# Two cross-attention layers: column sums by block transposes and one 0/1 matmul, weights' sums by a column of ones

## The chip, the core and the metric

The kernel runs on one core of a Trainium2 chip. A core has TensorE (PE: matrix products and transposes, results in PSUM banks), VectorE (DVE), ScalarE (ACT), GpSimd (POOL) and SyncE (SP, here used to issue transfers), and 16 DMA engines. Every engine works through its own queue of instructions in order and waits for the others by semaphores. The metric is the time of one launch on the device in microseconds; lower is better. All data are fp32.

## What is computed

`x` is 8 x 100 x 1024, the context `ctx_512` is 8 x 1444 x 512. Two layers of single-head attention from `x` to the context; hidden width 1024. Cut to what matters:

```python
# layer 0
Q = x @ Wq + bq;  K = ctx @ Wk + bk;  V = ctx @ Wv + bv
w = softmax(Q @ K.T / 32, axis=-1)          # over the 1444 keys
x = x + (w @ V) @ Wo + bo
# layer 1, with weights of its own
w = softmax(q @ k.T / 32, axis=1)           # over the 100 queries
x = x + w @ v
out = (x - mean(x)) * rsqrt(var(x) + 1e-6) * gamma + beta
```

In layer 1 the softmax goes over the queries, so the weights of a query do not add up to 1 over the keys, and the value bias has to be multiplied with their sum.

## The kernel before

**Shape of the work.** The kernel never forms keys and values. It multiplies the weights first: `wqk0` = Wq Wk^T (1024 x 512), `wvo` = Wv Wo (512 x 1024), `wqk1`; then the queries times these (`queries`), scores of the queries against the raw context, the weighted rows of the context, and a projection. A weight product is done by `weight_products` (L187) as seven half-size products X, Z, Y, W and so on, whose operands are sums and differences formed on VectorE (`combine`, L135), and whose results ScalarE copies (`put`, L242) and VectorE adds (L247). The body (L376 on) does qk0, vo0, the queries of layer 0, qk1, then layer 0's attention for eight batches, the projection `project0`, the queries of layer 1, and layer 1's attention with its projections and the final normalisation.

**Order.** PE runs in the order in which the program is written (`manual_schedule(engines={PE})`). The instructions of the other engines are put in order by the framework's planner. SP issues nearly all loads. They go into a ring of ten buffers, `unit` (L72), 128 x 1536 elements each: weight rows first, then, for each batch, four units of context columns (`cT`) and four of context rows (`c`, three chunks of 120 rows of 512 elements, `load_rows`, L429). A load waits until PE has used what the buffer held before.

**Biases.** Four vectors come out of biases and weights: u (bq by Wk), wqbk (bk by Wq), for each layer, and for the output bias bv by Wo. `accumulate` (L251) multiplies each of the eight 128-row slices of a weight with a column of the bias and adds them up on VectorE, which leaves an accumulator of 128 partitions by 512 or 1024 columns. Its sum over the partitions is wanted, laid out as a column of 128 partitions for each 128 columns. `totals` (L301) does that: PE transposes each 128 x 128 block into a PSUM bank, and VectorE reduces along the free axis (L308). The key bias of layer 0, `c0`, is the same with `key_bias_sums` (L323): VectorE adds up xT times wqbk over the eight chunks for 400 tokens at once, and the sums over partitions are taken by eight transposes in L400. `bias_product` (L311) multiplies bq and bk and sums them over partitions with a matmul by ones, once for each layer. ScalarE adds the output bias to xT in L406.

**Attention of layer 0.** `scores0` (L475) makes the scores of one batch in 11 pieces of 131 or 132 keys, 3 in a bank, 44 matmuls; ScalarE takes them out (L501), VectorE the maxima (L502), and the softmax goes on in ScalarE. VectorE transposes the weights by 32 x 32 blocks (L523). For batches 0 and 7 PE transposes the first four chunks (`first_transposed`, L533). `weighted_rows` multiplies the context rows by the weights (L458, 48 matmuls). In the loop of L800 a batch's weighted rows alternate on PE with the scores of the batch two ahead; batches 0 and 1 have their scores alone (L794 to L799).

**Attention of layer 1.** `scores1` (L603) and `attend1` (L659) alternate in the same way. `attend1` multiplies w (100 queries as columns) by context rows, four matmuls of 128 columns for each of 12 chunks, into one bank from the second pool of PSUM; batches 6 and 7 use `weighted_rows`. `weight_sums` (L632) adds the weights over the chunks on VectorE, and `weight_totals` (L643) transposes the result on PE and reduces it to the sum for each query, `r`, which `untransposed` multiplies with the value bias (L731).

**The end.** `normalise` (L739) has mean and variance, a power on GpSimd for `rstd` (L745), and for the last batch two VectorE instructions of 512 columns (L754), each followed by a DMA (L755), one issued by SP, one by ScalarE.

Of the kernel before, what the change touches and what calls it, by code (L numbers as in the profile page):

```python
# [30 lines left out]
P = 128  # L31
# [10 lines left out]
CUTS = [S * n // NP for n in range(NP + 1)]  # L42
QD = 32
# [10 lines left out]
def two_layer_cross_attention(ctx: ExitStack, tc: tile.TileContext, a: dict, out: bass.AP):  # L54
# [17 lines left out]
    def unit(name):  # L72
        return stream.tile([P, E + L], F32, tag="unit", name=name)
# [18 lines left out]
    make_identity(nc, ident)  # L92
    mhalf = const.tile([P, 1], F32, tag="mhalf", name="mhalf")
# [93 lines left out]
    def weight_products(name, left, right, l_width, r_width, scaled):  # L187
# [10 lines left out]
        if name == "qk0":  # L198
# [3 lines left out]
            for h in range(1, EC):  # L202
                nc.sync.dma_start(out=units[h][:, :lh], in_=lsrc[:, h, :lh])
                nc.sync.dma_start(out=units[h][:, l_width:], in_=rsrc[:, h, :])
                if h == 1:
                    nc.sync.dma_start(out=units[0][:, l_width + rh :], in_=rsrc[:, 0, rh:])
# [3 lines left out]
        else:  # L210
            for h in range(EC):
                nc.sync.dma_start(out=units[h][:, :l_width], in_=lsrc[:, h, :])
                nc.sync.dma_start(out=units[h][:, l_width:], in_=rsrc[:, h, :])
# [37 lines left out]
        def accumulate(side):  # L251
            for v, of in scaled:
# [8 lines left out]
                for h in range(EC):  # L261
                    src = units[h][:, :l_width] if side == 0 else units[h][:, l_width:]
# [38 lines left out]
    def totals(name, acc, n):  # L301

        got = const.tile([P, n], F32, tag=name, name=name)
        for c in range(0, n, 4):
            ps = bank(f"{name}_{c}")
            for i in range(4):
                nc.tensor.transpose(ps[:, i * P : (i + 1) * P], acc[:, (c + i) * P : (c + i + 1) * P], ident)
            nc.vector.tensor_reduce(got[:, c : c + 4], ps.rearrange("p (c q) -> p c q", q=P), AX.X, ALU.add)  # L308
        return got

    def bias_product(layer):  # L311

        prod = small.tile([P, EC], F32, tag="bb", name=f"bb{layer}")
        nc.vector.tensor_tensor(prod, cols[f"L{layer}_xattn_bq"], cols[f"L{layer}_xattn_bk"], ALU.mult)
        part = small.tile([P, 1], F32, tag="bbs", name=f"bbs{layer}")
        nc.vector.tensor_reduce(part, prod, AX.X, ALU.add)
        ps = bank(f"bb_ps{layer}")
        nc.tensor.matmul(ps[:, 0:1], ones, part, start=True, stop=True)
        got = const.tile([P, 1], F32, tag=f"bqbk{layer}", name=f"bqbk{layer}")
        nc.vector.tensor_scalar(got, ps[:, 0:1], SCALE, None, ALU.mult)  # L320
        return got

    def key_bias_sums(name, t0, t1, wqbk):  # L323

        acc = work.tile([P, GT], F32, tag="kb", name=name, bufs=3)
        for k in range(EC):
            src = xT[:, k, t0:t1]
            if k == 0:
                nc.vector.tensor_scalar(acc, src, wqbk[:, k : k + 1], None, ALU.mult)
            else:  # L330
                nc.vector.scalar_tensor_tensor(acc, src, wqbk[:, k : k + 1], acc, ALU.mult, ALU.add)
# [53 lines left out]
    bqbk0 = bias_product(0)  # L385
    bqbk1 = bias_product(1)
    wvo, (acc_o,) = weight_products("vo0", "L0_xattn_WvT", "L0_xattn_Wo", L, E, (("L0_xattn_bv", 1),))
    u0 = totals("u0", acc_u, LC)
    wqbk0 = totals("wqbk0", acc_c, EC)
    nc.vector.tensor_tensor(out_bias, out_bias, totals("bvo", acc_o, EC), ALU.add)  # L390
    gT = [queries(0, wqk0, u0), None]
# [4 lines left out]
    c0 = const.tile([T, B], F32, tag="c0", name="c0")  # L396
    for g in range(B // G):
        ps = bank(f"c0_ps{g}")
        for i in range(G):
            nc.tensor.transpose(ps[:T, i * P : (i + 1) * P], kb0[g][:, i * T : (i + 1) * T], ident)  # L400
        nc.vector.tensor_reduce(
            c0[:, g * G : (g + 1) * G], ps[:T].rearrange("p (b q) -> p b q", q=P), AX.X, ALU.add
        )
    nc.vector.tensor_scalar(c0, c0, SCALE, bqbk0[:T], ALU.mult, ALU.add)
# [492 lines left out]
```

## Time and profile before

| | |
|---|---|
| median of three runs | 653.13 us (653.09 to 653.53) |
| the profiled execution | 653.41 us, its span 651.6 us |
| granted TensorE clock | 0.996 of full speed |
| busy in the span | PE 641.9, DVE 401.1, ACT 128.2, POOL 39.3 us |
| moved by DMA | 127.51 MB, 196 GB/s in the mean |

The profile is one execution. It gives the busy time of each engine, a row of 40 equal slices of the span (16.3 us each) in which a digit is the busy share in tenths, groups of instructions (line, engine, operation, destination <- source, partitions x elements, count | busy us, mean ns | idle time before), and the chain of work that ended last, followed back from the last instruction. A timeline lists single instructions with their start and length, and in brackets how long the engine had been idle before and what it was waiting for. PE is the multiplication itself, PEld the loading of its stationary operand, which overlaps it.

### The profile page before, as it was taken

How to read it: one execution, taken by the hardware profiler on the slowest of the kernel's cores; microseconds unless marked ns; L12 is line 12 of the kernel's file. 1: busy time of each engine (PE TensorE's matmuls, PEld its weight loads, DVE VectorE, ACT ScalarE, POOL GpSimd, SP SyncE). 2: the span in 40 equal slices, each digit the busy share in tenths (PEclk: the TensorE clock that was granted, in tenths of full speed). 3: DMA queues.
4: the chain of work that ended last, by engine and by line, in shares of the span. 5: the costliest groups of instructions: out<-in, count | busy, mean ns of one | idle time of the engine just before them, and what ended most of it. 6: DMA issues, size and time to landing. Idle time of an engine off the chain costs nothing.

```text
span 651.6 us, 10319 instructions
## 1 busy us (share of the span) xinstructions
PE 641.9 (99%) x4272; PEld 544.1 (84%) x4272; DVE 401.1 (62%) x764; ACT 128.2 (20%) x320; POOL 39.3 (6%) x44
## 2 busy tenths in 40 slices
PE   9999999999999999999999999999999999999994
PEld 7886445568899999999998555589999999999992
DVE  4979737996145775576662875268344433556984
ACT  1010010330203333312320000204232222310221
POOL 5000000000000000000000000000000000000763
PEclk9999999999999999999999999999999999999998
DMA  8937037000089788998999003029799998920122
GB/s 292 387 107 288 0 94 287 2 0 2 0 319 305 266 316 297 322 318 305 329 357 340 0 0 130 1 95 282 262 306 294 305 316 294 309 95 1 51 76 76
DMA packets 60236, 127.51 MB, mean 196 GB/s; under 512 B 3929, under 2 KB 22873, under 8 KB 60189
## 3 DMA queue, kind: packets, MB, share of 16 engines
q1 hardware_dynamic: 57742, 119.82, 53.9%
q0 software_dynamic: 2048, 6.56, 3.0%
q8 instruction: 33, 0.54, 0.3%
q10 hardware_dynamic: 398, 0.47, 0.2%
q14 instruction: 15, 0.11, 0.1%
HBM read 123.56 MB, written 3.28 MB: 195 GB/s over the span
## 4 chain that ended last, share of the span: by engine, by line
PE 58%; issue 35%; POOL 4%; DMA 1%; SPq 0%; POOLq 0%; ACT 0%; DVE 0%; DVEq 0%
PE A L458 12%; PE s L488 12%; PE qk_x L124 6%; PE qk_y L124 4%; PE vo_x L124 3%; PE o_x L124 3%; POOL z L749 3%; PE g_x L124 3%; PE qk_w L124 2%; PE qk_z L124 2%; PE vo_y L124 2%; PE g_y L124 2%; PE o_y L124 1%; PE vo_w L124 1%; PE vo_z L124 1%
## 5 line engine op out<-in xcount | busy, mean ns | idle before, releaser
L458 PE MATMUL A<-w,c 120*128 120x100 f32 x960 | 145.0, 267 | 0.0
L458 PEld LDWEIGHTS A<-w,c 120*128 120x128 f32 x960 | 130.1, 191 | 0.0
L603 PE MATMUL s<-g1T,cT 128*120 128x100 f32 (+1 forms) x768 | 123.2, 262 | 0.0
L488 PE MATMUL s<-cT,g0T 128*100 128x131 f32 (+1 forms) x704 | 119.5, 275 | 0.0
L659 PE MATMUL A<-c,w 120*100 120x128 f32 (+1 forms) x576 | 110.7, 273 | 0.0
L603 PEld LDWEIGHTS s<-g1T,cT 128*120 128x120 f32 (+1 forms) x768 | 105.2, 185 | 0.6 <-issue 0.3
L488 PEld LDWEIGHTS s<-cT,g0T 128*100 128x100 f32 x704 | 87.1, 167 | 0.0
L523 DVE STREAM_TRANSPOSE w<-prob 32x384 f32<-32x384 f32 (+1 forms) x128 | 68.6, 536 | 15.3 <-ACT prob L509 12.5
L659 PEld LDWEIGHTS A<-c,w 120*100 120x100 f32 (+1 forms) x576 | 74.0, 168 | 0.0
L623 ACT ACTIVATE w<-w,negmax 120x100 f32<-120x100 f32 (+1 forms) x96 | 35.1, 366 | 75.3 <-DVE negmax L621 75.3
L613 DVE SCALAR_TENSOR_TENSOR w<-s,c 120x400 f32<-120x400 f32 (+1 forms) x24 | 13.8, 573 | 41.7 <-PE s L603 41.7
L501 ACT ACTIVATE prob<-s,c 100x394 f32<-100x394 f32 (+2 forms) x32 | 17.8, 562 | 97.0 <-PE s L488 96.8
L124 PE MATMUL qk_x<-qk 128*128 128x256 f32 x128 | 29.3, 385 | 0.4 <-DMA qk<-in_L_xattn_WkT 0.4
L502 DVE TENSOR_REDUCE maxima<-prob 100x1 f32<-100x394 f32 (+2 forms) x32 | 16.2, 527 | 21.5 <-ACT prob L501 21.2
L124 PEld LDWEIGHTS qk_x<-qk 128*128 128x128 f32 x128 | 24.1, 193 | 5.1 <-issue 1.2
L626 DVE RECIPROCAL rtotal<-total 120x4 f32<-120x4 f32 (+1 forms) x24 | 4.2, 176 | 28.2 <-ACT w L623 28.2
L745 POOL TENSOR_TENSOR rstd<-rstd,mhalf 100x1 f32<-100x1 f32 x8 | 7.5, 934 | 216.5 <-DVE rstd L744 216.4
L545 DVE TENSOR_TENSOR xT<-xT,o_x 128x400 f32<-128x400 f32 (+1 forms) x24 | 13.7, 603 | 8.3 <-PE o_x L124 7.9
L818 POOL DMA_DIRECT2D prob<-in_L_xattn_beta x1 | 0.5, 546 | 296.9 <-DVE w L523 296.9
L623 ACT ACTIVATION_READ_ACCUMULATOR w<-w,negmax 120x1 f32 (+1 forms) x96 | 17.9, 187 | 0.0
L266 DVE SCALAR_TENSOR_TENSOR qk_L_xattn_bk<-qk,L_xattn_bk,qk_L_xattn_bk 128x1024 f32<-128x1024 f32 x14 | 17.8, 1274 | 0.0
L640 DVE TENSOR_REDUCE part<-w 120x100 f32<-120x1100 f32 x8 | 17.2, 2144 | 0.0
(204 smaller groups left out, 894.1 us busy)
## 6 DMA issues: line engine op xcount, KB each, us to landing
c<-in_ctx SPq DMA_DIRECT2D x48, 768.0 KB, 7.4
cT<-in_ctxT SPq DMA_DIRECT2D x32, 728.0 KB, 6.6
cT<-in_ctxT SPq DMA_DIRECT2D x32, 722.0 KB, 6.3
c<-in_ctx SPq DMA_DIRECT2D x16, 512.0 KB, 8.8
vo<-in_L_xattn_Wo SPq DMA_DIRECT2D x8, 512.0 KB, 7.1
qk<-in_L_xattn_WqT SPq DMA_DIRECT2D x8, 512.0 KB
qk<-in_L_xattn_WqT SPq DMA_DIRECT2D x15, 256.0 KB, 5.4
qk<-in_L_xattn_WkT SPq DMA_DIRECT2D x15, 256.0 KB, 6.3
```

The costliest lines, as they stand in the source:

```text
L124: nc.tensor.matmul(banks[n // per][:, n % per * width : (n % per + 1) * width], lhs[i][:, n * P : (n + 1) * P], rhs[i], start=(fresh and i ...
L266: nc.vector.scalar_tensor_tensor(acc, src, cols[v][:, h : h + 1], acc, ALU.mult, ALU.add)
L458: nc.tensor.matmul(ps[:, k * T : (k + 1) * T], c[m // CQ][:r, m % CQ, k * P : (k + 1) * P], w[:r, m, :], start=(m == 0 and k == 0), stop=( ...
L488: nc.tensor.matmul(banks[n // PM][:T, CUTS[n] - o : CUTS[n + 1] - o], q0[:, k, t0 : t0 + T], cT[k][:, CUTS[n] : CUTS[n + 1]], start=(k == ...
L501: nc.scalar.activation(p[:, o:e], ps[:T, : e - o], AF.Identity, bias=c0[:, b : b + 1], scale=SCALE)
L502: nc.vector.tensor_reduce(parts[:, n : n + 1], p[:, o:e], AX.X, ALU.max)
L523: nc.vector.transpose(blocks(w, r, m0 * T + q * QD, T, MC - m0), blocks(p, q, m0 * MR + r * QD, MR, MC - m0),)
L603: nc.tensor.matmul(ps[:r, (m - m0) * T : (m - m0 + 1) * T], cT[m // CQ][:, k, o : o + r], q1[:, k, t0 : t0 + T], start=(k == 0), stop=(k = ...
L623: nc.scalar.activation(w[:r, m, :], w[:r, m, :], AF.Exp, bias=negmax[:r, m : m + 1], accum_out=total[:r, m : m + 1])
L640: nc.vector.tensor_reduce(part[:MR], w[:MR, :last, :].rearrange("p c t -> p t c"), AX.X, ALU.add)
L659: nc.tensor.matmul(ps[:T, part], w[:r, m, :], c[m // CQ][:r, m % CQ, part], start=(m == 0 and k == 0), stop=(m == MC - 1), skip_group_chec ...
L749: nc.gpsimd.tensor_tensor(z, z, beta[:T], ALU.add)
```

## The change

- **Sums over partitions.** `totals` takes no accumulator any more. `block_sums` transposes the accumulator in place on VectorE by 32 x 32 blocks and reduces each block's rows, which leaves for each partition p and each 32-column block the sum over one quarter of the partitions. One matmul with `same` (1 where two partitions agree modulo 32) adds the quarters, and VectorE keeps of each group the value that belongs to the partition (`quarter`, a 0/1 mask) and reduces. `same` and `quarter` are made from the identity at the start. u0 has a matmul of its own ahead of the queries; wqbk0 and the output bias share one, behind the queries; c0 has one; u1 and wqbk1 share one.
- **Key bias.** The operations for layer 0's key bias follow the queries, since wqbk0 does. Their accumulators are 28 columns longer, filled with zeros by GpSimd.
- **Bias products** of both layers share one matmul.
- **Output bias** is added to xT by GpSimd instead of ScalarE.
- **Scores alone.** For batches 0 and 1, `scores0` makes four pieces of 361 keys, each in a bank; the first transposes of batch 0 come before the last two matmuls.
- **Weights' sums.** A unit becomes three chunks of 513 columns. In layer 1's batches 0 to 5 GpSimd fills the last column with ones ahead of the load, and `attend1`'s fourth matmul takes 129 columns, into a bank of its own, so that its last column is `r`; ScalarE copies the two parts of A and r out. `weight_sums` and `weight_totals` remain for batches 6 and 7.
- **The end.** VectorE does 768 columns in one instruction, ScalarE and GpSimd the other 256.

The diff at its core:

```diff
-        return stream.tile([P, E + L], F32, tag="unit", name=name)
+        return stream.tile([P, CQ * (L + 1)], F32, tag="unit", name=name)
...
+    same = const.tile([P, P], F32, tag="same", name="same")
+    parts = ident.rearrange("p (r j) -> p j r", j=QD)
+    nc.vector.tensor_reduce(
+        same.rearrange("p (q j) -> p q j", j=QD),
+        parts.unsqueeze(1).to_broadcast([P, P // QD, QD, P // QD]),
+        AX.X,
+        ALU.add,
+    )
+    quarter = const.tile([P, P // QD], F32, tag="quarter", name="quarter")
+    nc.vector.tensor_reduce(quarter, ident.rearrange("p (r j) -> p r j", j=QD), AX.X, ALU.add)
...
-    def totals(name, acc, n):
+    def block_sums(name, t, sums):
+        nc.vector.transpose(t, t)
+        nc.vector.tensor_reduce(sums, t.rearrange("p (c q i) -> p c q i", q=P // QD, i=QD), AX.X, ALU.add)
+
+    def totals(name, sums, n):
+        ps = bank(name)[:, : n * P // QD]
+        nc.tensor.matmul(ps, same, sums.rearrange("p c q -> p (c q)"), start=True, stop=True)
+        own = small.tile([P, 2 * EC, P // QD], F32, tag="own", name=f"{name}_own", bufs=1)[:, :n, :]
+        mask = quarter.unsqueeze(1).to_broadcast([P, n, P // QD])
+        nc.vector.tensor_tensor(own, ps.rearrange("p (c q) -> p c q", q=P // QD), mask, ALU.mult)
         got = const.tile([P, n], F32, tag=name, name=name)
-        for c in range(0, n, 4):
-            ps = bank(f"{name}_{c}")
-            for i in range(4):
-                nc.tensor.transpose(ps[:, i * P : (i + 1) * P], acc[:, (c + i) * P : (c + i + 1) * P], ident)
-            nc.vector.tensor_reduce(got[:, c : c + 4], ps.rearrange("p (c q) -> p c q", q=P), AX.X, ALU.add)
+        nc.vector.tensor_reduce(got, own, AX.X, ALU.add)
         return got
...
-    bqbk0 = bias_product(0)
-    bqbk1 = bias_product(1)
+    bqbk0, bqbk1 = bias_products()
     wvo, (acc_o,) = weight_products("vo0", "L0_xattn_WvT", "L0_xattn_Wo", L, E, (("L0_xattn_bv", 1),))
-    u0 = totals("u0", acc_u, LC)
-    wqbk0 = totals("wqbk0", acc_c, EC)
-    nc.vector.tensor_tensor(out_bias, out_bias, totals("bvo", acc_o, EC), ALU.add)
-    gT = [queries(0, wqk0, u0), None]
+    sums_u = quarter_sums("u0")[:, :LC, :]
+    block_sums("u0", acc_u, sums_u)
+    sums_c = quarter_sums("c0")
+    block_sums("wqbk0", acc_c, sums_c[:, :EC, :])
+    gT = [queries(0, wqk0, totals("u0", sums_u, LC)), None]
+    block_sums("bvo", acc_o, sums_c[:, EC:, :])
+    got = totals("wqbk0", sums_c, 2 * EC)
+    wqbk0 = got[:, :EC]
+    nc.vector.tensor_tensor(out_bias, out_bias, got[:, EC:], ALU.add)
...
+    sums = quarter_sums("kb0")[:, :B, :]
+    t = row("kbT").rearrange("p (b q j) -> p b q j", q=P // QD, j=QD)
     for g in range(B // G):
-        ps = bank(f"c0_ps{g}")
-        for i in range(G):
-            nc.tensor.transpose(ps[:T, i * P : (i + 1) * P], kb0[g][:, i * T : (i + 1) * T], ident)
...
+        src = bass.AP(kb0[g].tensor, kb0[g].offset, [list(kb0[g].ap[0]), [T, G], [QD, P // QD], [1, QD]])
+        nc.vector.transpose(t[:, g * G : (g + 1) * G], src)
+    nc.vector.tensor_reduce(sums, t, AX.X, ALU.add)
+    c0 = totals("c0", sums, B)
+    nc.vector.tensor_scalar(c0, c0, SCALE, bqbk0, ALU.mult, ALU.add)
     for e in range(EC):
-        nc.scalar.activation(xT[:, e, :], xT[:, e, :], AF.Identity, bias=out_bias[:, e : e + 1])
-    u1 = totals("u1", acc_u, LC)
-    wqbk1 = totals("wqbk1", acc_c, EC)
+        nc.gpsimd.tensor_scalar(xT[:, e, :], xT[:, e, :], out_bias[:, e : e + 1], None, ALU.add)
+    sums = quarter_sums("k1")
+    block_sums("u1", acc_u, sums[:, :LC, :])
+    block_sums("wqbk1", acc_c, sums[:, LC : LC + EC, :])
+    got = totals("k1", sums[:, : LC + EC, :], LC + EC)
...
+            if summed:
+                nc.gpsimd.memset(t[:, :, L:], 1.0)
...
-    def scores0(s, cT):
+    def scores0(s, cT, alone=False):
...
+        n_pieces, per = (NB, 1) if alone else (NP, PM)
...
-        ps = bank2(f"A1_{b}")
+        whole, rest = bank2(f"A1_{b}"), bank(f"A1r_{b}")
...
+                to = rest[:T, : P + 1] if k == LC - 1 else whole[:T, k * P : (k + 1) * P]
...
-                    c[m // CQ][:r, m % CQ, part],
+                    c[m // CQ][:r, m % CQ, k * P : (L + 1 if k == LC - 1 else (k + 1) * P)],
...
-        for j in range(2):
-            w = slice(j * E // 2, (j + 1) * E // 2)
-            nc.vector.scalar_tensor_tensor(z[:, w], z[:, w], rstd, beta[:T, w], ALU.mult, ALU.add)
-            (nc.scalar if j else nc.sync).dma_start(out=out[b][:, w], in_=z[:, w])
+        w, rest = slice(0, 3 * E // 4), slice(3 * E // 4, E)
+        nc.scalar.activation(z[:, rest], z[:, rest], AF.Copy, scale=rstd)
+        nc.gpsimd.tensor_tensor(z[:, rest], z[:, rest], beta[:T, rest], ALU.add)
+        nc.vector.scalar_tensor_tensor(z[:, w], z[:, w], rstd, beta[:T, w], ALU.mult, ALU.add)
+        nc.sync.dma_start(out=out[b][:, w], in_=z[:, w])
+        nc.scalar.dma_start(out=out[b][:, rest], in_=z[:, rest])
```

## The prediction, made before the changed kernel ran

> **What bounds the kernel now.** I read the totals and the 40 slices first, then PE's waits, then the chain of waits, then the timeline where the change touches it.
>
> ```profile
> PE 641.9 (99%) x4272; PEld 544.1 (84%) x4272; DVE 401.1 (62%) x764; ACT 128.2 (20%) x320; POOL 39.3 (6%) x44
> PE   9999999999999999999999999999999999999994
> DVE  4979737996145775576662875268344433556984
> DMA  8937037000089788998999003029799998920122
> ```
>
> TensorE (PE) is full in every slice but the last, at a granted clock of 0.996. The list of PE's waits names two things in the whole run: 1.1 us for the first memset and 0.4 us for the first loads. So a PE instruction removed shortens the run by its length, and work on other engines costs nothing unless it makes PE late. Columns of the chain: start, length, engine, destination, line, records (a matmul of fp32 leaves two, a transpose one).
>
> ```profile
> 54.74 0.34 PE bb_ps L318 x4
> ...
> 103.34 0.44 PE u L307 x4
> 103.78 0.87 PE wqbk L307 x8
> 104.65 0.87 PE bvo L307 x8
> ...
> 191.85 0.87 PE c_ps L400 x8
> 192.73 0.44 PE u L307 x4
> 193.16 0.88 PE wqbk L307 x8
> 194.04 18.95 PE s L488 x168
> ...
> 232.96 1.09 PE A L458 x10
> ```
>
> The first seven rows are what the change takes off PE in the first 194 us: all lie on the chain, back to back with products.
>
> **PE's own work.** Removed: 0.34 + 0.44 + 0.87 + 0.87 + 0.87 + 0.44 + 0.88 = 4.71 us. Added: one matmul for both bias products (half of 0.34, so 0.17), and four with the block matrix `same`, of 16, 64, 32 and 48 columns. Nearest rows: the one-column matmul at 0.17, the 100-column A at 1.09/5 = 0.218. I take 0.2 each: 0.97 with the first. Net **-3.74** (between -3.9 and -3.6).
>
> `weight_totals` loses six of its eight transposes in layer 1, 0.109 each as in the u row: -0.65. In exchange `attend1`'s fourth matmul has 129 columns instead of 128, in 12 chunks of six batches: 72 columns. The half products give the slope: 0.859 us at 512 columns, 0.432 at 256, so 1.67 ns a column, +0.12. The s pieces (131 columns, begun at odd columns) take 18.95/84 = 0.2256, which is 131 x 1.67 + 7 ns, so an odd width or start has no visible price. Net **-0.53**.
>
> `scores0` for batches 0 and 1 has 16 matmuls of 361 columns (361 x 1.67 + 7 = 0.61 us) instead of 44 of 131: 9.71 against 9.93, twice: **-0.43**. The transposes of batch 0's first chunks now stand two matmuls before the end of batch 1's scores. Batch 0's last score ends 9.7 us after the first one's start, the softmax needs 4.8 more (204.0 to 208.7 now), and PE reaches the transposes at 9.71 + 14 x 0.607 = 18.2: 3.7 us of cover; if it were gone, PE would wait for the difference.
>
> **The end of the run.**
>
> ```profile
> 644.90 1.52 POOL L745 TENSOR_TENSOR rstd<-rstd,mhalf 100x1 f32<-100x1 f32 x1 [4.20 <-DVE rstd L744]
> 646.46 1.41 DVE L754 SCALAR_TENSOR_TENSOR z<-z,rstd,prob 100x512 f32<-100x512 f32 x2 [0.46 <-POOL rstd L745]
> ...
> 647.91 0.57 ACTq L755 DMA_DIRECT2D out<-z  x1
> ```
>
> Now two VectorE (DVE) instructions run after rstd (646.42), and ScalarE's DMA goes out at 647.91. After, DVE has one of 768 columns: L746 does 1024 in 1.27, so about 1.0, DMA at 647.55. The other 256 go ScalarE, then GpSimd: 256/1024 of 1.15 (L748) and of 2.36 (L749) with 0.15 fixed each gives 0.4 + 0.75, and ScalarE's DMA at about 647.7. Sum -0.2 to -0.4 if they don't disturb each other, +0.5 if GpSimd and DVE hold each other up; I take **-0.25**.
>
> **VectorE in front of the first products.** `same` and `quarter` are two new reductions on DVE, ahead of everything that needs them; in DVE's order they come between two accumulations of the query bias.
>
> ```profile
> 12.57 0.75 DVE L266 SCALAR_TENSOR_TENSOR qk_L_xattn_bq<-qk,L_xattn_bq,qk_L_xattn_bq 128x512 f32<-128x512 f32 x1 [0.77 <-DMA qk<-in_L_xattn_WkT]
> ...
> 19.86 1.16 PEld L124 LDWEIGHTS qk_y<-qk_s 128*128 128x128 f32 x6 [0.40 <-DVE qk_s L135]
> ```
>
> DVE idles 0.77 us there. 512 elements cost 0.68 by the contiguous reductions of L308 and 1.08 by L640 (strided, 1.8 ns an element); the small one 0.28. So 0.96 to 1.36 into 0.77: DVE is 0.2 to 0.6 later. The rows behind go through to PE, since Y's first weights load already waits 0.40 for `qk_s`. I take **+0.35** (0 to 0.6).
>
> **VectorE elsewhere, costed at nothing.** The block transposes and reductions of u0 and wqbk0 are 0.70 + 0.68 + 1.24 + 1.22 = 3.85 us (by w's transposes, 1.05 ns an element + 0.17, and L308's rate) and stand where DVE waits 4.17 us for Wo:
>
> ```profile
> 47.09 0.69 DVE L135 TENSOR_TENSOR vo_s<-vo 128x512 f32<-128x512 f32 x1 [4.17 <-DMA vo<-in_L_xattn_Wo]
> 86.13 2.03 DVE L135 TENSOR_TENSOR g_t<-xT 128x400 f32<-128x400 f32 x4 [8.99 <-PE vo_x L124]
> ```
>
> bvo's go into the 8.99 before 86.13. Without that cover the combination at 47 would be up to 2 us late, and PE with it. The sixteen key-bias operations of layer 0, 8.4 to 10 us, move behind the queries, to 143-152, with u0 no longer behind wqbk0 on PE. Behind them on DVE stand qk1's operands; PE asks for W's at 162 and for the next X's at 169, and they would be ready at about 155 and 164.5: 4 us or more of cover, then a 1:1 stall. DVE has 18.6 us idle at 165-184, which also takes the sums for c0, u1 and wqbk1 (some 9 us by the same rates) before PE asks for them at 191; without that gap PE would wait for them at the end of qk1. The six weight sums (6 x 2.9 us) leave DVE, which has no wait on PE's path there. Bank `A1r` is held for a whole batch, leaving five to the scores, which take three a batch, and one for the transposes of A: no allocation comes to it; if one did, PE would wait for an eviction, 0.57 us by L613's mean.
>
> Here a rule speaks against the change. The row first: L746 averages 1651 ns where GpSimd is often at work and takes 1274 alone. The Trainium skill, "SBUF — State Buffer", "Who interferes with whom", has DVE's second read and write port shared with GpSimd under an exclusive lock. GpSimd's eight new bias adds (800 elements, an estimated 0.9 to 1.8 us each, the latter by L749) follow the second half of the key-bias operations and then run beside two-input subtractions. By the rows, a stretch of 1.3 on some 10 us, +3, is covered; by the rule, up to 14 us of lock could leave W's operands 7 us late. I go with the row.
>
> **Transfers.** All row loads (47 of 127.5 MB) now land in rows of 513 columns, 2052 bytes apart. Columns below: stretch, sum, busy PE, PEld, DVE, ACT, POOL, clock, DMA share, GB/s.
>
> ```profile
> 234.00:254.00 20.00, 20.00 (x190) 20.00 (x189) 12.34 (x25) 5.34 (x7) 0.00 (x0) 1.00 0.90 308
> 475.00:497.00 22.00, 22.00 (x216) 22.00 (x215) 9.93 (x19) 5.74 (x26) 0.00 (x0) 1.00 0.92 302
> 327.00:354.00 27.00, 27.00 (x245) 27.00 (x244) 9.23 (x22) 3.78 (x5) 0.56 (x2) 1.00 1.04 357
> ```
>
> The attention stages move 302-308 GB/s where 357 was reached. The Trainium skill, "DMA: Bandwidth & Descriptors", "How a descriptor splits into AXI transactions", counts a transfer begun off a 256-byte line as extra 32-byte beats: estimated 65 to 72 instead of 64 for 2048 bytes, +6% on average if it holds for the written side, 3% on the stage: 0.90 becomes 0.93. By row and by rule: nothing, and the price of more is the third case below. No row here has a transfer or a weights load from 2052-byte rows; `A` loads 128 columns in 0.19 us under 0.22 of s.
>
> In layer 1, 24 row loads on SyncE's queue wait for GpSimd's memset of the ones column, itself waiting for PE to release the buffer: 0.3 to 0.5 us later each (an estimate from GpSimd's small rows), with the next cT load behind on the queue. Batch 2's first rows land at 491.4 and are used at 497: hidden. At 389 GpSimd's DMAs for wv, bv1, gamma and beta stand behind at most one memset, already free at 352.
>
> **Sum.** -3.74 - 0.53 - 0.43 - 0.25 + 0.35 = -4.6 us, on the profiled execution's 653.41 (span 651.6 and 1.8 around it): 648.8. That execution is 0.28 above the median, so **648.5** against 653.13, -0.7%.
>
> **The rivals.**
> - *Mine*, 0.70: 648.5, own range 647 to 649.8.
> - *VectorE gives some back*, 0.16: the moved key-bias operations and the port make qk1's W or X wait 1 to 3 us, or the Wo gap doesn't hold. For it: DVE's slices of 9 at 114-147 us; against: the 6 and 1 behind them. 649.5 to 651.7, about 650.5.
> - *Row loads bind*, 0.08, slower: in the sixteen attention batches (some 20 us each). From 0.90 the share reaches 1.0 when rows, half the bytes, cost 22% more; at 40% more the stage is at 1.08, +1.6 us a batch, 26 us less 4.6: 674. At 30%: 1.035, +0.7 x 16 = 11, so 660. It turns the sign at about 25%. Against: no shortage now, and buffers filled 5 us ahead.
> - *The memset hop binds the loads of layer 1*, 0.06: 24 x 0.17 us = 4.1 lost of 4.6, 652.6, no change. Against: the same 5 us.
>
> Less than 0.2% (1.3 us) can't be told from no change. Faster: 0.70 + 0.16 = 0.86; same 0.06; slower 0.08. The range leaves out the third case and reaches to the fourth's edge: **646.8 to 652.0**.
>
> **What would show it.** Right: the transposes of L307 and L400 gone and four short matmuls in the chain; g's first product at about 103.7 (2.52 off, 0.37 and 0.35 on) instead of 105.5, layer 0's scores at about 190.7 instead of 194.0; a batch of 19.6 us in layer 0 as now, and 0.09 shorter in six of layer 1. Wrong: PE waiting for DVE in qk1 or at vo; a longer batch with the DMA share near 1; the last DMA later after rstd than now (1.5 us).

## The result

The changed kernel takes 649.41 us in the median of four runs (649.17 to 649.94), the kernel before 653.33 in its four (653.09 to 654.22): a ratio of 0.9939, 95% interval 0.9921 to 0.9956. It is faster, by 3.9 us or 0.6%. The forecast was 648.5 with a range of 646.8 to 652.0. The profiled execution took 649.66 us with a span of 647.9, 3.7 us below the span before.

The totals and the slices of the changed kernel:

```profile
PE 637.1 (98%) x4120; PEld 530.4 (82%) x4120; DVE 395.9 (61%) x751; ACT 122.6 (19%) x325; POOL 64.0 (10%) x81
PE   9999999999999999999999999999999999999994
DVE  5999949569624775566753784266322223566984
DMA  8928028000099888898998002038889999920212
```

TensorE is as full as before and has 152 records fewer. GpSimd has 25 us more to do, VectorE only 5 us less: six weight sums are gone, but the bias sums came in their place. The slices of DMA are the same but for a digit here and there.

The chain of waits of the changed kernel, where the new matmuls stand (columns as in the prediction):

```profile
54.89 0.12 PE bb_ps L342 x2
...
103.26 0.13 PE u L323 x2
103.39 2.78 PE g_x L135 x8
...
141.38 0.17 PE wqbk L323 x2
...
190.03 0.14 PE c L323 x2
190.17 0.24 PE k L323 x2
...
190.41 18.29 PE s L528 x60
208.70 0.34 PE pT L578 x4
209.04 1.22 PE s L528 x4
```

40 transposes and two matmuls, 4.71 us in all, have become five short matmuls of 0.80 us, and the first score starts at 190.41 instead of 194.04.

To take the start of the run out of the comparison I read the starts of TensorE's stages from the trace, in us:

| from ... to | before | after | difference | the prediction's step |
|---|---|---|---|---|
| first Z product to first Y product of qk0 | 7.06 | 7.40 | +0.34 | +0.35 |
| first Y to the first score of layer 0 | 174.01 | 170.24 | -3.77 | -3.74 |
| first score to the projection of layer 0 | 160.21 | 159.87 | -0.34 | -0.43 |
| that projection to the first one of layer 1 | 219.59 | 219.08 | -0.51 | -0.53 |
| that to the last matmul | 69.78 | 69.77 | 0 | 0 |
| last matmul to the end of the span | 8.19 | 8.92 | +0.73 | -0.25 |

The sum is -3.6. The two spans differ by another 0.2 because Z itself began 0.19 earlier; that depends on when the first loads land. Over the fourteen profiled executions of this study Z began anywhere between 11.84 and 13.28 us, without relation to the edits, whereas the time from the first Y to the last matmul came out at 618.96 or 618.97 in eight executions of the changed kernel and of variants that leave TensorE's instructions alone and don't starve it (a ninth, with the masks made on GpSimd, has 618.86; see there). So differences of tenths are read below from stages, and the medians only show their sum.

Five of the six steps hold within 0.1 us. The last has the wrong sign, by 1 us. Its timeline in the changed kernel:

```profile
640.42 1.52 POOL L792 TENSOR_TENSOR rstd<-rstd,mhalf 100x1 f32<-100x1 f32 x1 [4.18 <-DVE rstd L791]
641.97 0.51 ACT L800 ACTIVATE z<-z,rstd 100x256 f32<-100x256 f32 x1 [9.07 <-POOL rstd L792]
641.98 1.02 DVE L802 SCALAR_TENSOR_TENSOR z<-z,rstd,prob 100x768 f32<-100x768 f32 x1 [0.46 <-POOL rstd L792]
642.56 1.01 POOL L801 TENSOR_TENSOR z<-z,prob 100x256 f32<-100x256 f32 x1 [0.62 <-ACT z L800]
643.02 0.31 SPq L803 DMA_DIRECT2D out<-z  x1
643.60 0.56 ACTq L804 DMA_DIRECT2D out<-z  x1
```

rstd is ready at 641.94. VectorE's 768 columns take 1.02 as forecast, so nothing held them up. GpSimd's 256 take 1.01 instead of 0.75, ScalarE's 0.51 instead of 0.4, and the last transfer goes out 1.66 us after rstd where it went out 1.48 after it before. That later issue is 0.18, and the loss is 0.73. The transfers' packets, under the experiments, tell where it comes from.

### The profile page after: what moved, and what is told of

It reads as the page before. It is cut to its first block, busy times and chain, and to the rows that moved or that the text cites. A ratio compares the mean times of both kernels' runs of the same rounds, so it can differ in the third digit from the quotient of the medians.

```text
span 647.9 us, 10121 instructions
## 1 busy us (share of the span) xinstructions
PE 637.1 (98%) x4120; PEld 530.4 (82%) x4120; DVE 395.9 (61%) x751; ACT 122.6 (19%) x325; POOL 64.0 (10%) x81
## 3 DMA queue, kind: packets, MB, share of 16 engines
q0 software_dynamic: 2048, 6.56, 3.1%
## 4 chain that ended last, share of the span: by engine, by line
PE 81%; issue 11%; POOL 4%; DMA 1%; DVE 1%; POOLq 0%; ACT 0%; SPq 0%
PE A L496 12%; PE s L528 12%; PE s L643 10%; PE A L703 6%; PE qk_x L135 5%; PE g_x L135 5%; PE qk_y L135 4%; PE g_y L135 3%; PE vo_x L135 3%; PE o_x L135 3%; POOL z L796 3%; PE qk_w L135 2%; PE vo_y L135 2%; PE A1r L703 2%; PE o_y L135 2%
## 5 line engine op out<-in xcount | busy, mean ns | idle before, releaser
L528 PE MATMUL s<-cT,g0T 128*100 128x131 f32 (+2 forms) x592 | 119.0, 296 | 0.0
L528 PEld LDWEIGHTS s<-cT,g0T 128*100 128x100 f32 x592 | 77.6, 167 | 8.3
L703 PE MATMUL A<-c,w 120*100 120x128 f32 (+1 forms) x432 | 83.0, 273 | 0.0
L563 DVE STREAM_TRANSPOSE w<-prob 32x384 f32<-32x384 f32 (+1 forms) x128 | 68.6, 536 | 15.3 <-ACT prob L549 12.5
L703 PEld LDWEIGHTS A<-c,w 120*100 120x100 f32 (+1 forms) x432 | 55.5, 168 | 0.0
L541 ACT ACTIVATE prob<-s,c 100x394 f32<-100x394 f32 (+3 forms) x32 | 18.0, 563 | 94.5 <-PE s L528 94.3
L438 POOL TENSOR_SCALAR xT<-xT,L_xattn_bo 128x800 f32<-128x800 f32 x8 | 20.8, 2610 | 133.3 <-PE qk_x L135 133.3
L542 DVE TENSOR_REDUCE maxima<-prob 100x1 f32<-100x394 f32 (+3 forms) x32 | 16.3, 527 | 24.1 <-ACT prob L541 23.8
L703 PE MATMUL A1r<-c,w 120*100 120x129 f32 x144 | 27.8, 274 | 0.0
L470 POOL MEMSET c<- 128x3 f32 x24 | 2.5, 104 | 162.7 <-PE s L643 140.0
L703 PEld LDWEIGHTS A1r<-c,w 120*100 120x100 f32 x144 | 18.5, 168 | 0.0
L585 DVE TENSOR_TENSOR xT<-xT,o_x 128x400 f32<-128x400 f32 (+1 forms) x24 | 13.7, 601 | 7.9 <-PE o_x L135 7.5
```

The source lines that it names most:

```text
L438: nc.gpsimd.tensor_scalar(xT[:, e, :], xT[:, e, :], out_bias[:, e : e + 1], None, ALU.add)
L528: nc.tensor.matmul(banks[n // per][:T, cuts[n] - o : cuts[n + 1] - o], q0[:, k, t0 : t0 + T], cT[k][:, cuts[n] : cuts[n + 1]], start=(k == ...
L541: nc.scalar.activation(p[:, o:e], ps[:T, : e - o], AF.Identity, bias=c0[:T, b : b + 1], scale=SCALE)
L542: nc.vector.tensor_reduce(parts[:, n : n + 1], p[:, o:e], AX.X, ALU.max)
L563: nc.vector.transpose(blocks(w, r, m0 * T + q * QD, T, MC - m0), blocks(p, q, m0 * MR + r * QD, MR, MC - m0),)
L703: nc.tensor.matmul(to, w[:r, m, :], c[m // CQ][:r, m % CQ, k * P : (L + 1 if k == LC - 1 else (k + 1) * P)], start=(m == 0 and k in (0, LC ...
```

## The experiments

### The end, taken back and transplanted

The changed kernel with the old end:

```diff
-        w, rest = slice(0, 3 * E // 4), slice(3 * E // 4, E)
-        nc.scalar.activation(z[:, rest], z[:, rest], AF.Copy, scale=rstd)
-        nc.gpsimd.tensor_tensor(z[:, rest], z[:, rest], beta[:T, rest], ALU.add)
-        nc.vector.scalar_tensor_tensor(z[:, w], z[:, w], rstd, beta[:T, w], ALU.mult, ALU.add)
-        nc.sync.dma_start(out=out[b][:, w], in_=z[:, w])
-        nc.scalar.dma_start(out=out[b][:, rest], in_=z[:, rest])
+        for j in range(2):
+            w = slice(j * E // 2, (j + 1) * E // 2)
+            nc.vector.scalar_tensor_tensor(z[:, w], z[:, w], rstd, beta[:T, w], ALU.mult, ALU.add)
+            (nc.scalar if j else nc.sync).dma_start(out=out[b][:, w], in_=z[:, w])
```

> The changed kernel with the end of the kernel before: two VectorE instructions of 512 columns, each with its DMA. From the last matmul's end to the end of the span the profile has 8.1 us before the change and 8.9 after it. Theory (the new end costs 0.8 us): 8.1 to 8.2 us here, span about 647.1, 0.75 us shorter than the changed kernel. Rival (the two ends differ by accident of one execution): 8.9 here as well, or any value between.

Measured: 8.12 us behind the last matmul. The span, 647.9, is not shorter than the changed kernel's: in this execution Y began at 20.87 instead of 20.00, and that took up what the end gave (648.99 us in the median of four). From the first Y on it is the theory's 0.8.

The kernel before with the same lines exchanged the other way:

> The kernel before with the new end alone (VectorE 768 columns, ScalarE and GpSimd 256). Theory: 8.9 us from the last matmul to the end of the span instead of 8.1, so 0.8 us slower than before. Rival (the end is longer only in company with the rest of the change, such as another order on GpSimd): 8.1 us, no difference.

Measured: 9.01 us behind the last matmul, and 653.85 us in the median of twelve runs against 653.23 for the kernel before on the same chip, ratio 1.0008 (1.0000 to 1.0017). The new end is a loss by itself: 0.82 us in its stage, which the medians alone would hardly show.

### Why the end is slower: the cut of the transfers

```diff
-        nc.sync.dma_start(out=out[b][:, w], in_=z[:, w])
-        nc.scalar.dma_start(out=out[b][:, rest], in_=z[:, rest])
+        nc.sync.dma_start(out=out[b][:, : E // 2], in_=z[:, : E // 2])
+        nc.scalar.dma_start(out=out[b][:, E // 2 :], in_=z[:, E // 2 :])
```

> The changed kernel with the new end's computation, but the transfers cut at column 512: SyncE's carries 512 columns behind the 768 of VectorE, ScalarE's the other 512 behind VectorE and GpSimd. Theory (most of the loss is that the late transfer's packets come behind 3072-byte packets of the early one, 0.55 us; only 0.18 is the later issue): ScalarE's first packet about 1.1 us after its issue as before instead of 1.8, and 8.3 to 8.4 us from the last matmul to the end. Rival (the loss is lateness of the issue alone, or of the GpSimd instruction): 8.9 us as now.

Measured: 8.46 us behind the last matmul. The packets of the two output transfers, in us after rstd was ready (100 packets each):

| | bytes, early / late | early: issue, packets | late: issue, packets | behind the last matmul |
|---|---|---|---|---|
| before | 2048 / 2048 | 0.81, 1.59 to 2.99 | 1.48, 2.62 to 3.80 | 8.19 |
| changed | 3072 / 1024 | 1.08, 1.87 to 4.10 | 1.66, 3.43 to 4.53 | 8.92 |
| cut at 512 | 2048 / 2048 | 1.08, 1.87 to 3.25 | 1.66, 2.88 to 4.06 | 8.46 |

The issues of the changed kernel and of this one are the same to the hundredth, and so is the computation; only the cut of the bytes differs. It moves the late transfer's first packet by 0.55 us and the end by 0.46. In each row the late packets begin only when the early transfer has 0.37 or 0.67 us left. So of the 0.73 us, 0.46 is the large early transfer (most of its packets take 121 ns instead of 84). The other 0.27 is the delay of the early transfer's issue, 1.08 instead of 0.81, since VectorE now does 768 columns before it and not 512; the 0.18 by which the late issue is later does not come on top, as its packets wait anyway. An early transfer ends with ten packets of 4 bytes, and the first late packet follows the first of these closely: 2.57 and 2.62 before, 3.42 and 3.43 in the changed kernel, 2.84 and 2.88 with the cut at 512. So I read it that an engine takes up the late transfer when it is through with the early one; which engine carries a packet, the trace does not tell.

The old end with its queues exchanged (ScalarE issues the first half, SyncE the second):

```diff
-            (nc.scalar if j else nc.sync).dma_start(out=out[b][:, w], in_=z[:, w])
+            (nc.sync if j else nc.scalar).dma_start(out=out[b][:, w], in_=z[:, w])
```

> The changed kernel with the old end, and the queues exchanged: ScalarE issues the first half, SyncE the second. Issues take 0.57 us on ScalarE and 0.31 on SyncE, and the first packet comes 1.14 and 0.78 us after the issue. Theory (the late transfer should stand on the queue that starts it sooner): 7.8 us from the last matmul to the end. Rival (the late packets wait for the early ones, whichever queue): 8.1 us as in the old end, or more if the early half is now late.

Measured: 8.16 us behind the last matmul, so the rival is right and my theory is not. The first packet comes 0.82 us after ScalarE's issue and 1.18 after SyncE's: the wait belongs to the second transfer, not to the queue.

### Are the row loads of layer 1 short of time?

```diff
-                nc.gpsimd.memset(t[:, :, L:], 1.0)
+                nc.gpsimd.memset(t, 1.0)
```

> The changed kernel, but in layer 1's batches 0 to 5 GpSimd fills the whole unit with ones ahead of each row load instead of its last columns (128 x 1539 elements, about 1.3 us by the 32 x 1448 fills at the start, instead of 0.1). From the first half product Y of qk0 to the last matmul TensorE takes 623.60 us before the change and 618.96 after it. Theory (the loads have slack): 618.96 still, with a batch of 20.27 us. Rival (the hop from TensorE over GpSimd to SyncE's queue is all that the loads can bear): up to 24 x 1.2 = 29 us more.

Measured: 618.96 us from the first Y to the last matmul, exactly as in the changed kernel. The group's row:

```profile
L470 POOL MEMSET c<- 128x1539 f32 x24 | 33.2, 1382 | 134.5 <-PE s L643 116.0 <-PE A L496 7.9 <-DMA cT<-in_ctxT 6.7
```

24 fills of 1.38 us stand between the release of a buffer and its load, and TensorE never waits. The hop that I priced at 4.1 us in all has room for at least thirteen times its length (0.104 us in the changed kernel).

### GpSimd beside VectorE

The output bias back on ScalarE:

```diff
-        nc.gpsimd.tensor_scalar(xT[:, e, :], xT[:, e, :], out_bias[:, e : e + 1], None, ALU.add)
+        nc.scalar.activation(xT[:, e, :], xT[:, e, :], AF.Identity, bias=out_bias[:, e : e + 1])
```

> The changed kernel with the output bias of layer 0 added by ScalarE as before, so that GpSimd does nothing beside VectorE's key-bias operations. These average 751 ns in the changed kernel (626 in layer 1's, with GpSimd idle). Theory (GpSimd stretches VectorE, but under cover): 620 to 640 ns each here, and TensorE from the first Y to the last matmul at 618.96 as in the changed kernel. Rival (the stretch reaches TensorE): shorter by 0.1 us or more.

Two groups of the changed kernel, GpSimd's adds and the key-bias operations beside them:

```profile
L438 POOL TENSOR_SCALAR xT<-xT,L_xattn_bo 128x800 f32<-128x800 f32 x8 | 20.8, 2610 | 133.3 <-PE qk_x L135 133.3
...
L356 DVE SCALAR_TENSOR_TENSOR kb<-xT,wqbk,kb 128x400 f32<-128x400 f32 x14 | 9.5, 751 | 0.0
```

The same operations with the bias on ScalarE:

```profile
L356 DVE SCALAR_TENSOR_TENSOR kb<-xT,wqbk,kb 128x400 f32<-128x400 f32 x14 | 7.7, 628 | 0.0
```

628 instead of 751 ns in the mean, and TensorE's time from the first Y to the last matmul stays 618.96: both as the theory had it. But the mean of 751 hides two kinds of instruction. The row of the line alone, in the changed kernel (shortest, median and longest in ns, then the first and last start in us):

```profile
L356 DVE SCALAR_TENSOR_TENSOR kb<-xT,wqbk,kb x14: 621/622/1221, 143.2 to 152.1; 128x400 f32<-128x400 f32 x14
```

Eleven of the fourteen take 0.62 us, as without GpSimd, and three take 1.22. The three begin 0.6 to 0.8 us behind the start of GpSimd's first, second and third add. Read singly, six of the eight adds hold up one instruction of VectorE with two inputs in SBUF, by 0.4 to 0.7 us each, 3.4 us together; the other two hold up none. GpSimd gives way too: an add takes 2.28 us alone and up to 2.99 beside such instructions. So it is not a stretch but a wait, once for each add.

The rows from which the prediction took its stretch, L746 of the kernel before, show a longer wait. Single instructions of that kernel's timeline:

```profile
629.38 1.27 DVE L746 SCALAR_TENSOR_TENSOR z<-z,mv,prob 100x1024 f32<-100x1024 f32 x1
632.34 2.36 POOL L749 TENSOR_TENSOR z<-z,prob 100x1024 f32<-100x1024 f32 x1 [1.26 <-ACT z L748]
633.99 1.78 DVE L746 SCALAR_TENSOR_TENSOR z<-z,mv,prob 100x1024 f32<-100x1024 f32 x1
```

The second L746 begins while GpSimd's addition is under way and ends 1.08 us after it (635.77 and 634.70). Five of the eight L746 begin in this way; they take 1.46 to 2.68 us, and each ends 1.08 us after GpSimd's addition, in this execution as in the other thirteen (1.08 or 1.09). So they wait until GpSimd is through.

The adds doubled:

```diff
+    half_bias = const.tile([P, EC], F32, tag="half_bias", name="half_bias")
+    nc.vector.tensor_scalar(half_bias, out_bias, 0.5, None, ALU.mult)
     for e in range(EC):
-        nc.gpsimd.tensor_scalar(xT[:, e, :], xT[:, e, :], out_bias[:, e : e + 1], None, ALU.add)
+        for _ in range(2):
+            nc.gpsimd.tensor_scalar(xT[:, e, :], xT[:, e, :], half_bias[:, e : e + 1], None, ALU.add)
```

> The changed kernel with GpSimd's bias adds doubled: sixteen adds of half the bias, about 41 us from 143 to 185 instead of 21, so that GpSimd runs beside VectorE until the end of qk1's additions. Theory (a stretch of 1.2 of VectorE's work, as the measured rows show): qk1's operands 1 to 2 us later, covered, TensorE's 618.96 us unchanged or longer by at most 0.5. Rival (VectorE and GpSimd exclude each other): 2 to 7 us longer.

```profile
156.70 38.04 POOL L441 TENSOR_SCALAR xT<-xT,half_bias 128x800 f32<-128x800 f32 x16 [146.58 <-DVE half_bias L438]
```

The planner put the halving of the bias behind the key-bias operations, so the 38 us of adds began at 156.7 and not at 143: they stand beside qk1's subtractions and not beside the key-bias sums, which are back at 626 ns. It is not quite the load that I meant, but a longer one beside the operands that TensorE needs next. Six of the sixteen adds hold up one instruction of VectorE each, by 0.5 to 0.7 us, and TensorE's 618.96 us are unchanged.

### How much DMA headroom is there?

One more load of 128 KB, never used, for each row load of layer 0 (17% on the rows). It goes to a buffer `more` of 128 x 512; `second` turns true behind layer 0:

```diff
             t = unit(f"c_{b}_{q}").rearrange("p (c l) -> p c l", c=CQ)
+            for h in (q % 2,) if not second[0] else ():
+                nc.sync.dma_start(out=more[h * 64 : h * 64 + 64, :], in_=src[q * QR + h * 64 : q * QR + h * 64 + 64, :])
```

> The changed kernel with one more load of 128 KB (64 rows of 2048 bytes, never used) for each row load of layer 0's eight batches, 17% on the rows and 9% on all that the stage moves. DMA share there is 0.88 in the changed kernel. Theory (a sum of shares: the stage binds only above 22% more on the rows): share about 0.96, layer 0's attention as long as before (from the first score to the first half product of the projection: 159.87 us). Rival (the loads are already just in time and the queue feels any addition): some us longer.

Measured: 159.87 us, unchanged. The share, from 231 to 271 us, is 0.88 at 305 GB/s and not 0.96. The same with `range(2)` in place of `(q % 2,)`, 33% on the rows:

> The changed kernel with two more loads of 128 KB for each row load of layer 0: 33% on the rows, 17% on all that the stage moves. Theory of the prediction (shares add up: 0.88 becomes 1.03 and every batch is stretched): layer 0's attention 159.87 us becomes about 165. Rival (the ring of ten buffers has rows in place some 15 us before use; with 17% more the lead fell to 7-9 us at the last batch, so what the DMA engines lack is paid from the lead first): no wait before batch 5 or 6, and 0 to 4 us in all.

Measured: 175.42 us, 15.6 longer. Both expectations are far too small. TensorE's waits in layer 0's second half, and a table by stretches (columns as in the prediction):

```profile
PE s L530 <- DMA cT<-in_ctxT: 6.2, 3, 2.4
PE A L498 <- DMA c<-in_ctx: 3.0, 2, 2.8
```

```profile
231.00:271.00 40.00, 40.00 (x378) 40.00 (x377) 23.93 (x46) 11.73 (x15) 0.00 (x0) 1.00 0.98 316
271.00:311.00 40.00, 40.00 (x377) 40.00 (x376) 24.09 (x47) 11.23 (x16) 0.60 (x1) 1.00 1.00 312
...
350.00:360.00 10.00, 7.20 (x46) 7.04 (x44) 0.00 (x0) 0.00 (x0) 0.00 (x0) 0.74 0.90 276
360.00:370.00 10.00, 10.00 (x37) 8.10 (x37) 2.69 (x6) 0.00 (x0) 0.10 (x1) 0.57 1.06 375
```

There is no wait before 300 us. Then TensorE waits 9.2 us in five places, and around the last and longest of these (2.8 us, to 355.4) the granted clock is 0.74 and 0.57 in the mean: the trace's record of the clock has half speed from 354.9 to 368.5. That goes with the other 6 (the stage after it is 1.4 us longer too). The rival had the place right, and neither had the clock.

The same stretch of the changed kernel:

```profile
231.00:271.00 40.00, 40.00 (x378) 40.00 (x377) 23.93 (x46) 11.75 (x15) 0.00 (x0) 1.00 0.88 309
```

A share of 0.88 and one of 0.98 differ by 7 GB/s of 309. It would be rash to conclude that the engines can give no more. All added loads write the one buffer `more`, so each waits in SyncE's queue until an earlier one has landed, and the loads behind it in the queue wait too. The longest entry among the waits of SyncE's queue in the 33% run, from 200 to 350 us (total, times, longest):

```profile
SPq L470 <- DMA more<-in_ctx: 65.4, 24, 4.9
```

With 17% more it is 16.2 us in 7 waits. And with 17% more the engines gave 333 GB/s at a share of 1.02 from 271 to 311 us, where the 33% run has 312. So whether bytes or these waits made the loads late is open, and with it how much headroom there is.

What both runs show is what keeps TensorE supplied, the lead of the loads. The four row loads of batch 7 land 14.7 to 15.3 us before their first use in the changed kernel and 6.6 to 6.9 us before it with 17% more. With 33% more the first lands 0.1 us before it, and TensorE waits for the second and the third.

### The weights' sums as before

`attend1`, `weight_sums` and `weight_totals` for all eight batches as in the kernel before, rows still 513 columns apart:

```diff
-        whole, rest = bank2(f"A1_{b}"), bank(f"A1r_{b}")
+        ps = bank2(f"A1_{b}")
...
-        c, *cT = loaded(load_rows(b, nxt), *([load_columns(b + 2)] if nxt else []))
+        c, *cT = loaded(load_rows(b), *([load_columns(b + 2)] if nxt else []))
...
-        if not nxt:
-            weight_totals(batches[b])
+        weight_totals(batches[b])
...
-        if B - 3 <= b < B - 1:
+        if b + 1 < B:
```

> The changed kernel with the weights' sums as before: no ones column, attend1 into one bank with 128 columns, sums on VectorE and a transpose on TensorE for all eight batches; all else as changed, rows still 513 columns apart. Theory (six transposes of 0.109 against 72 columns of 1.67 ns, nothing else): from the first Y to the last matmul 618.96 + 0.53 = 619.5 us. Rival (the ones column has costs of its own on TensorE, by the waits for a bank or by rows that come later): 619.0 or less.

Measured: 619.48 us, 0.52 more than the changed kernel. The ones column is worth six transposes less 72 columns and has no other cost on TensorE.

### The scores in eleven pieces

```diff
-    run(scores0(batches[0], *loaded(load_features(0)), alone=True))
-    s0 = scores0(batches[1], *loaded(load_features(1)), alone=True)
-    for n in range(LC * NB):
+    run(scores0(batches[0], *loaded(load_features(0))))
+    s0 = scores0(batches[1], *loaded(load_features(1)))
+    for n in range(LC * NP):
         next(s0)
-        if n == LC * NB - 3:
+        if n == LC * NP - 4:
             first_transposed(batches[0])
```

> The changed kernel with the scores of batches 0 and 1 in 11 pieces of 131 columns again instead of four of 361; the first transposes stand three matmuls before the end. Theory of the prediction (7 ns a matmul beside its columns): 0.43 us longer, 619.39 from the first Y to the last matmul. Rival (read from the changed kernel's chain, 0.61 us a matmul of 361 and 19.51 against 19.85 us for both batches): 0.34 longer, 619.30.

Measured: 619.51, 0.55 more, which fits neither. The stage itself tells why: before the change, with four matmuls behind the transposes, it is 0.34 longer than after it; here three are behind them.

```profile
208.81 0.51 PE L578 MATMUL pT<-ident,prob 100*120 100x100 f32 x4
209.15 0.84 PE L528 MATMUL s<-cT,g0T 128*100 128x131 f32 x6
209.35 0.49 ACT L579 COPY w<-pT 120x400 f32<-120x400 f32 x1 [0.21 <-PE pT L578]
...
209.90 0.47 PE L496 MATMUL A<-w,c 120*128 120x100 f32 x2
```

ScalarE's copy of the transposed weights ends at 209.84, and the first A, which reads it, begins at 209.90, right behind it. The score that follows the two A begins 20.60 us after the stage's first score, where it began 20.40 after it in the kernel before: 0.20 is lost here. In the changed kernel A begins 0.4 us after the copy's end, so two matmuls of 361 columns are more than enough. The 0.34 of the pieces and the 0.20 of this wait add up to the 0.55.

### The masks on GpSimd, with the old end

```diff
-    nc.vector.tensor_reduce(
-        same.rearrange("p (q j) -> p q j", j=QD),
...
-    nc.vector.tensor_reduce(quarter, ident.rearrange("p (r j) -> p r j", j=QD), AX.X, ALU.add)
...
+    pairs = const.tile([P, P // 2], F32, tag="pairs", name="pairs")
+    nc.gpsimd.tensor_tensor(pairs, ident[:, : P // 2], ident[:, P // 2 :], ALU.add)
+    same = const.tile([P, P], F32, tag="same", name="same")
+    halves = [pairs[:, h * QD : (h + 1) * QD].unsqueeze(1).to_broadcast([P, P // QD, QD]) for h in range(2)]
+    nc.gpsimd.tensor_tensor(same.rearrange("p (q j) -> p q j", j=QD), *halves, ALU.add)
+    quarter = const.tile([P, P // QD], F32, tag="quarter", name="quarter")
+    nc.gpsimd.memset(quarter, 0.0)
+    for q in range(P // QD):
+        nc.gpsimd.memset(quarter[q * QD : (q + 1) * QD, q : q + 1], 1.0)
```

and the old end as above.

> The changed kernel with two things altered: the end of the kernel before (two halves on VectorE), and the two mask matrices made on GpSimd (two additions and five fills) instead of by two VectorE reductions in front of the first Y. Theory: 8.1 us behind the last matmul instead of 8.9, and Y's wait for VectorE 0.1 to 0.3 us shorter: 0.8 to 1.1 us below the changed kernel, 648.4 in the median. Rival (the masks fill idle time of VectorE and cost nothing): 0.8 only; their gain can't be told from the 0.7 us by which the first loads vary from one execution to the next.

Measured: 648.33 us (647.94 to 648.83), ratio to the kernel before 0.9926 (0.9913 to 0.9940): the fastest version of the study, 1.1 us below the median of the changed kernel. It ends 8.11 us behind the last matmul. From Z to Y it takes 6.91 us instead of 7.40, and from Y to the last matmul 618.86 instead of 618.96: Y itself is 0.10 shorter where its operands don't have to be waited for. In the changed kernel the waits of the weight loads and of the matmuls have these lines, which are missing here:

```profile
PEld qk_y L135 <- DVE qk_s L146: 0.7, 1, 0.7
```

```profile
PE qk_y L135 <- DVE qk_s L146: 0.3, 1, 0.3
```

How much the masks cost depends on when the loads land: in the other executions with the masks on VectorE the stage takes 7.09 to 8.01 us, mostly 7.40, and in the two of kernels with the old start 6.98 and 7.06. So like has to be compared with like. In this execution VectorE waits for no load from 8 us to the start of Y. The same holds for three with the masks on VectorE that start as early (the cut at 512, the doubled adds, the eleven pieces): Y's operand is ready at 19.30 or 19.31 us and Y begins at 19.36 or 19.37; here it is ready at 18.91 and Y begins at 19.20. That is 0.16 us, with the 0.10 within Y 0.26: the theory holds, from one execution of this version. By the medians alone the rival could not have been excluded.

## Why the prediction was right, and where it was not

**TensorE's own work: right.** The sums of biases were put at -3.74 and measured -3.77: the short matmuls take 0.12 to 0.24 us where 0.17 to 0.2 was assumed. The weights' sums were put at -0.53, the run without the ones column shows 0.52. The scores of batches 0 and 1 were put at -0.43 and measured -0.34: a matmul of 361 columns takes 0.610 us. The prediction's own formula, 361 x 1.67 + 7 ns, says so too; its sum was made with 0.607, and 32 times 3 ns are a quarter of so small a gain.

**VectorE in front of the first Y: right in kind**, and taken away by the masks on GpSimd. The two reductions take 1.05 and 0.28 us as the rows had it, and the accumulation behind them begins at 12.85 instead of 12.57, 0.28 late. That +0.34 was measured where +0.35 was forecast is luck: in this pair of executions Y began 0.14 later and Z 0.19 earlier, and other executions with the masks have +0.02 to +0.95 against the same 7.06.

**The end of the run: wrong, and the only wrong sign.** The step "I take -0.25" has -0.4 to +0.5 as its ends; it measured +0.73, outside both. What failed is that I put the end at the issue of the last transfer, as if the time from there were the same. The run with the transfers cut at 512 shows that 0.46 of the 0.73 comes from the bytes in the early transfer; the other 0.27 is the early transfer's own issue, which is that much later. The late issue was mis-sized too, 1.66 us after rstd instead of about 1.28, but its first packet came only at 3.43, when the early transfer was nearly done. Part of this lateness is GpSimd's addition, 1.01 us instead of 0.75 (a quarter of the row with 0.15 fixed gives 0.70). I had taken that VectorE and GpSimd don't hold each other up, and they do: GpSimd's power for rstd (L745, L792) always begins beside VectorE's instruction of 1024 columns and always ends 0.42 to 0.47 us after it, so it takes 1.52 us in the last batch and 0.58 where it begins late. The addition of 256 columns likewise ends 0.58 us after VectorE's 768. With the 0.46 us of the 128-column addition in the run with the masks on GpSimd and the 2.36 of 1024 columns, I estimate 0.73 for 256 columns alone. No run moved VectorE's instruction away, so for this addition the wait is argued and not shown. The upper end of +0.5 had this reason, but it is not what made the end longer.

The steps ahead of the last matmul gave 4.3 us where 4.35 was forecast; the end is what the result misses of the forecast's 4.6.

**VectorE elsewhere, costed at nothing: right, from a row misread.** TensorE waits for VectorE only at the first Y. I read the mean of L746, 1651 ns against 1274, as a stretch of 1.3 and set it against the rule of the Trainium skill ("SBUF — State Buffer", "Who interferes with whom"), the exclusive lock. The single instructions of that row follow the rule: they wait until GpSimd's addition is through. Beside the new adds the wait is shorter than the rule's whole instruction, 0.4 to 0.7 us of 2.28 or more, and why it is shorter stays open. So the up to 14 us of lock did not come, and that the adds cost VectorE 3.4 us where the stretch gave 3 is luck. GpSimd's adds were mis-sized: 2.28 us alone and 2.61 in the mean, not 0.9 to 1.8.

**Transfers: the result right, the reasoning not.** Rows 2052 bytes apart cost nothing that can be seen: a stage of layer 0 has a share of 0.88 after and 0.90 before, not the 0.93 of the rule. But "the attention stages move 302-308 GB/s where 357 was reached" does not tell how much is free: with 17% more on the rows one stretch kept its share of 0.88, and what was lacking was taken from a lead of 15 us, not 5. My price of the third rival, 0.7 us a batch at 30%, is wrong in form: in the run with 33% more there is nothing until the lead is used up, then 9.2 us of waits and 6 more with the clock in a single layer. Where its turning point lies is not shown, since the added loads of that run waited for one another. The fourth rival, the memset in front of the loads, is excluded by the 1.38 us fills.

## What to carry to other kernels

When TensorE bounds a kernel and the chain of waits shows it back to back, the sum of removed and added matmuls, at durations read from neighbouring rows, is good to 0.1 us. At the end of the run count up to the last byte, not to the last issue: of two transfers the second started when the first had 0.4 to 0.7 us left, so the early one must not be the large one. A ring of buffers hides late loads until its lead is spent; read the lead, not the share of busy DMA engines. A mean over a row can hide a wait: before you call a longer mean a stretch, read the single instructions. And loads added to test the DMA engines need buffers of their own.

## What the runs showed that I had not expected

- The first packet of the second of two output transfers came 1.14 to 1.77 us after its issue, that of the first always 0.78 to 0.82, whichever of the queues of SyncE and ScalarE had which.
- In the run with 33% more on the rows TensorE waited 9.2 us between 300 and 355 us, none of these waits longer than 2.8; the granted clock was then 0.5 for 13.7 us, though TensorE had work again from 355.4 on. Together this cost 17 us from the first Y to the last matmul.
- In both kernels the last batch's rstd takes GpSimd 1.52 us where 0.58 is seen in others, because VectorE's instruction of 1024 columns goes first. That is 0.94 us at the end of the run; no run here tried another order.
- From the first Y on, 619 us of TensorE's time repeat to 0.01 us in eight executions; what varies is the start, where Z begins anywhere in 1.4 us and Y in 1.7.
